# One batch's MLP split between two product forms, two exchange targets, and dense work laid out by units

## The chip, the cores and the metric

The kernel runs on one core of a Trainium2 chip, in one launch. The metric is the time of that launch in microseconds on the device; the table below has the median of three runs and one execution that was taken with the profiler. The five engines have their own instruction streams: PE (TensorE, with its weight loads as PEld), DVE (VectorE), ACT (ScalarE), POOL (GpSimd) and SP (SyncE), whose queue issues nearly all transfers.

## What is computed

A cross-attention block with its MLP, in float32: four batches of 512 tokens, 512 channels, 16 heads of 32, an MLP of 2048.

```python
residual = hidden_states
x = layer_norm(hidden_states, ln1_w, ln1_b)
q = (x @ q_w + q_b).reshape(B, LQ, H, HD).transpose(0, 2, 1, 3)
k = (encoder_hidden_states @ k_w + k_b).reshape(B, LK, H, HD).transpose(0, 2, 1, 3)
v = (encoder_hidden_states @ v_w + v_b).reshape(B, LK, H, HD).transpose(0, 2, 1, 3)
scores = jnp.einsum('bhqd,bhkd->bhqk', q, k) * scale
scores = jnp.where(mask, scores, mask_value)
attn = jax.nn.softmax(scores, axis=-1)
out = jnp.einsum('bhqk,bhkd->bhqd', attn, v)
out = out.transpose(0, 2, 1, 3).reshape(B, LQ, D)
out = out @ cproj_w + cproj_b
hidden = out + residual
residual = hidden
y = layer_norm(hidden, ln2_w, ln2_b)
y = jax.nn.gelu(y @ fc_w + fc_b, approximate=True)
y = y @ proj_w + proj_b
return residual + y
```

## The kernel before

**Units.** Attention runs over 16 groups `w` (four batches of four groups of four heads), and in each over four query tiles `qt` of 128 tokens. One (w, qt) is a unit, numbered u = 4w + qt from 0 to 63. `scores` has PE make four 128 x 512 score tiles in one four-bank PSUM tile, `sc`, of which there is one; DVE adds the mask and takes the row minimum (L244, scores are negated) into one of six `s` tiles; ACT takes the exponential with its sum (L248). `turn` has DVE transpose the four tiles in 32 x 32 blocks into `tb`. After the second unit of a pair (a half of a group's queries) DVE and ACT add the reciprocal sums, and `exchange` sends `tb` to a target tile, `pT`, by 16 transfers from SP's queue (`copies`), which move the blocks between partition quarters. `attend` then has PE multiply by the values (`av`) and DVE scale into `oT` (L327).

**Targets.** Pairs in `IN_G` go to `gt` and pairs in `IN_XE` to `xe`; all others go to the one `pT` tile, and then an exchange waits in a list until the pair before it has been attended (`held`). Pair p is attended before the scores of unit 2p + 4 (`LAG`), except for those in `AT`. `tb` has two buffers.

**Dense work.** Products of 128 x 512 x 512 are called chains: `prep_k`, `prep_q`, `prep_v` make a group's keys, queries and values, `cproj` is the attention's output projection of 128 tokens, `fc` and `proj` are the MLP's two halves in quarters of its 2048 channels. Each is four matmuls of 512 columns (sixteen of 128 in `prep_v`), a PSUM tile from a ring of four (`acc`) and an evacuation: by ACT for keys, queries, values and gelu, by DVE for cproj and proj. Lists `first[w]` and `later[w]` name the work of a group in order, with a cost (3.4 for a chain, 0.5 for a transpose step, 0 for vector work), and the loop spreads a group's list over its four units by an even share of that cost. `some(n)` takes the next n chains of the MLP. PE, DVE, ACT and SP run everything in the order in which it is written (a manual schedule).

**The MLP.** `NORMAL = 2`: batches 0 and 1 have all their MLP as chains, in the groups from 5 on and behind the loop, eight weight tiles in a ring (`load_mlp`). Batches 2 and 3 are done after attention in `last_mlps` with seven products of quarter blocks in place of eight (`fc_pair`, `project`): sums of weight blocks (`sum_wa`, `p_sums`), of activation blocks (`y_sums`, `g_sums`) and of results are made by DVE, ACT and POOL. A product there is two or sixteen matmuls of 256 columns.

**Layer norms.** `ln_stat` and `ln_norm` run on DVE, `ln_rs` on POOL; `ln_turn` transposes on PE and applies weight and bias on ACT (d = 0, 3) and DVE (d = 1, 2). `load_h` brings a batch's x again for the residual; batches that do not stay in SBUF go through DRAM (`xa`, `load_hid`).

The parts that order the work around the change are these:

```python
first[0] = [(CHAIN, lambda: prep_v(1))] + x2[:1] + [(CHAIN, lambda: prep_q(1))] + x2[1:2] + [k2] + x2[2:] + [k3, v2]
...
later[4] = c[:1] + x2[:1] + c[1:2] + x2[1:2] + c[2:3] + x2[2:] + c[3:] + stat(0, 0, 1, 2, 3) + rs(0)
first[5] = x3[:2] + [k] + x3[2:] + norm(0, 0, 1, 2, 3) + [v] + t2[:2] + [q] + t2[2:] + pb_(0) + some(5)
```

Of the kernel before, what the change touches and what calls it, by code (L numbers as in the profile page):

```python
# [43 lines left out]
P = 128  # L45
# [13 lines left out]
NORMAL = 2  # L59
LAG = 4  # L60
IN_G = (1, 3, 5, 7)
IN_XE = (29, 31)
AT = {5: 0, 7: 1, 9: 2, 11: 3, 13: 4, 15: 5, 17: 6}
# [10 lines left out]
def xattn_block(ctx: ExitStack, tc: tile.TileContext, x, encT, mask, q_w, k_w, v_w, c_w, fc_w, p_w, vecs, rows, out):  # L74
# [11 lines left out]
    one, two, kqp, five, six, fws = pools(att, one=1, two=2, kqp=4, five=5, six=6, fws=MW)  # L86
# [16 lines left out]

    S = {}
    Q = [nc.sync]
# [12 lines left out]
    def ln_rs(key):  # L118

        ve = small.tile([P, NT], F32, tag="ve", name=f"ve{key[0]}_{key[1]}")  # L120
        nc.gpsimd.tensor_scalar(ve, S["mv", key][:, :, 1], EPS, 1.0, ALU.add, ALU.mult)
        rs = small.tile([P, NT], F32, tag="rs", name=f"rs{key[0]}_{key[1]}")
        nc.gpsimd.tensor_tensor(rs, ve, nhalf, ALU.pow)
        S["rs", key] = rs

    def ln_norm(key, t, dst, src):
        nc.vector.tensor_scalar(
            dst, src, S["mv", key][:, t, 0:1], S["rs", key][:, t : t + 1], ALU.subtract, ALU.mult
        )

    def ln_turn(key, d, xn, dst):

        w, bi = (LN1W, LN1B) if key[0] == 1 else (LN2W, LN2B)
        tp = acc_tile(f"tp{key[0]}_{key[1]}_{d}")
        for t in range(NT):
            nc.tensor.transpose(tp[:, ts(t, P)], xn[t][:, ts(d, P)], ident)
        wd, bd = vec[:, w + d : w + d + 1], vec[:, bi + d : bi + d + 1]
        if d in (1, 2):
            nc.vector.tensor_scalar(dst[:, d, :], tp, wd, bd, ALU.mult, ALU.add)
        else:  # L140
            nc.scalar.activation(dst[:, d, :], tp, AF.Identity, bias=bd, scale=wd)  # L141
# [38 lines left out]
    def load_w(w, queue=None, names=("wk", "wq", "wv")):  # L180

        if w >= NW:
            return
        g = w % NG
        for n, src in (("wk", k_w), ("wq", q_w), ("wv", v_w)):
            if n in names:
                S[n, w] = two.tile([P, ND, P], F32, tag=n, name=f"{n}_{w}")
                (queue or Q[0]).dma_start(out=S[n, w], in_=src[:, g, :, :])

    def prep_k(w):  # L190
        b, g = divmod(w, NG)
        kT = kqp.tile([P, L], F32, tag="kT", name=f"kT_{w}")
# [7 lines left out]
    def prep_q(w):  # L200
        b, g = divmod(w, NG)
        qT = kqp.tile([P, L], F32, tag="qT", name=f"qT_{w}")
# [29 lines left out]
    def scores(w, qt):  # L232
# [8 lines left out]
        for h in range(HG):  # L241
            s = six.tile([P, L], F32, tag="s", name=f"s_{w}_{qt}_{h}")
# [93 lines left out]
    def stays(b, t):  # L336

        return b == 0 or b < B - 1 and t < 2

    def load_h(b, *ts_):  # L340
# [3 lines left out]
        for t in ts_:  # L344
            pool, tag = (hids, "hid") if stays(b, t) else (tiles, "xn")
            S["h", b, t] = pool.tile([P, D], F32, tag=tag, name=f"h_{b}_{t}")
# [8 lines left out]
    def cproj(b, t):  # L355
# [5 lines left out]
        if not stays(b, t):  # L361
            (nc.sync if b == B - 1 else nc.gpsimd).dma_start(out=S["xa", b][ts(t, P), :], in_=h)

# [30 lines left out]
    for b in range(NORMAL):  # L394
        for name, q in (("fc", 0), ("fc", 1), ("p", 0), ("fc", 2), ("p", 1), ("fc", 3), ("p", 2), ("p", 3)):
# [4 lines left out]
    count = [0, 0]  # L400

    def load_mlp():

        while count[0] < len(weights) and (count[0] < MW or weights[count[0] - MW][3] < count[1]):
            name, b, f, _ = weights[count[0]]
            w = fws.tile([P, D], F32, tag="mw", name=f"{name}w_{b}_{f}")
# [67 lines left out]

    def last_mlps():
# [5 lines left out]
        pb = last.tile([P, NP, 2, D], F32, tag="pb", name="pb")  # L481
        pt = last.tile([P, 3, NP, HL], F32, tag="pt", name="pt")
        hl = last.tile([P, NT, D], F32, tag="hl", name="hl")
        p1p, u2p, u3p = (last.tile([P, 2, HL], F32, tag=n, name=n) for n in ("p1p", "u2p", "u3p"))
# [13 lines left out]
        def p_sums(c):  # L498

            c = slice(c, c + 2)  # L500
            b11, b12, b21, b22 = (pb[:, c, k, j * HL : (j + 1) * HL] for k in range(2) for j in range(2))
            b_sums(b11, b12, b21, b22, pt[:, 0, c], pt[:, 1, c], b12, pt[:, 2, c])

# [5 lines left out]
        def fc_pair(b, c, sums):  # L509
# [25 lines left out]
            if c == 0:  # L535
# [9 lines left out]
            if c:  # L545
# [6 lines left out]
        def project(b, sums, turns, middle):  # L552
# [5 lines left out]
            def product(o, a, w, ts_=range(2)):  # L558
                for t in ts_:
                    for c in range(NP):  # L560
                        nc.tensor.matmul(o[:, t], a[:, c, ts(t, P)], w[:, c], start=(c == 0), stop=(c == NP - 1))  # L561
# [47 lines left out]

        y_sums(NORMAL)  # L610
        for t in range(NT):
            S["hid", B - 1, t] = hl[:, t]
        for b in range(NORMAL, B):
            for c in range(NP):
                if b == NORMAL:
                    for i in range(2):
                        nc.sync.dma_start(out=pb[:, c, i, :], in_=p_w[ts(2 * c + i, P), :])
                fc_pair(b, c, lambda: sum_wa(c + 1) if c + 1 < NP else None)
# [4 lines left out]
                if c % 2 == 0 and c:  # L623
                    g_sums(c - 2)

                if b + 1 < B:
# [8 lines left out]
            def sums(b=b):  # L635
                if b == NORMAL:
                    for c in range(0, NP, 2):
                        p_sums(c)
# [3 lines left out]
            def turns(b=b):  # L642
                if b + 1 < B:
                    run(turns2(b + 1))

# [5 lines left out]
            project(b, sums, turns, middle)  # L651
# [64 lines left out]
    load_h(0, *range(NT))  # L716
    nc.sync.dma_start(out=wc, in_=c_w)
# [8 lines left out]
    run(x1)  # L726
    make_mb(0)
# [10 lines left out]
    first[0] = [(CHAIN, lambda: prep_v(1))] + x2[:1] + [(CHAIN, lambda: prep_q(1))] + x2[1:2] + [k2] + x2[2:] + [k3, v2]  # L738
    first[1] = [(CHAIN, lambda: (prep_v(3), load_enc(1)))] + [q2, q3] + x3[:2]
    first[2] = [k4] + x3[2:] + [v4, q4] + A(5)[:1]  # L740
    first[3] = A(5)[1:] + A(6)
    mlp = []
    for p in range(NORMAL):
        mlp += FC(p, 0) + FC(p, 1) + PJ(p, 0) + FC(p, 2) + PJ(p, 1) + FC(p, 3) + PJ(p, 2) + PJ(p, 3)

# [27 lines left out]
    first[3] += cb(0)  # L773
# [3 lines left out]
    later[4] = c[:1] + x2[:1] + c[1:2] + x2[1:2] + c[2:3] + x2[2:] + c[3:] + stat(0, 0, 1, 2, 3) + rs(0)  # L777
    k, q, v = A(8)
    first[5] = x3[:2] + [k] + x3[2:] + norm(0, 0, 1, 2, 3) + [v] + t2[:2] + [q] + t2[2:] + pb_(0) + some(5)
    k, q, v = A(9)  # L780
    x1, x2, x3, x4 = inputs(3)
    first[6] = [k, q] + some(5) + [v] + x1
    k, q, v = A(10)
    first[7] = [k, q] + x2[:1] + some(3) + x2[1:2] + some(3) + [v]
# [5 lines left out]
    first[9] = [q] + some(2) + [k] + some(3) + [v]  # L790
    k, q, v = A(13)
    first[10] = [k, q] + some(5) + [v]
    k, q, v = A(14)
    t2 = turns2(1)
    first[11] = stat(1, 0, 1) + [k, q] + stat(1, 2, 3) + rs(1) + some(2) + norm(1, 0, 1) + some(1)
    first[11] += norm(1, 2, 3) + some(2) + t2 + pb_(1) + [v]

    k, q, v = A(15)
    first[12] = h_(2, 2, 3, 0, 1) + [k] + some(3)
    later[12] = cb(2) + C(2)  # L800
    first[13] = hid_(1, 2, 3) + [q] + some(3) + [v] + some(3)
    first[14] = some(5) + stat(2, 0, 1) + some(2) + stat(2, 2, 3) + rs(2) + some(1)
    first[15] = norm(2, 0, 1) + some(4) + norm(2, 2, 3) + some(4) + turns2(2) + pb_(2)

    for w in range(NW):
        if w and w % NG == 0:
            make_mb(w // NG)
        work, rest = first[w], later[w]
        share = sum(c for c, _ in work + rest) / NT
        due = 0.0  # L810
        for qt in range(NT):
# [7 lines left out]
            turn(w, qt)  # L819

# [6 lines left out]
        run(work + rest)  # L827
    exchange()

    load_h(B - 1, *range(NT))  # L830
# [3 lines left out]
    load_wa(0)  # L834
    run(some(2))
    attend(NW - 1, 1)
    run(some(2))
    load_wa(1)
    sum_wa(0)
    c_bias(B - 1)  # L840
    run(C(B - 1))
    load_hid(NORMAL, (2, 3))
# [46 lines left out]
```

## Time and profile before

| | us |
|---|---|
| median of three runs (820.71 to 821.26) | 820.94 |
| the profiled execution | 818.4 |
| its span, first to last instruction | 816.6 |
| PE busy | 798.2 |
| DVE busy | 546.8 |
| ACT busy | 354.6 |
| POOL busy | 90.5 |

Busy time is not a sum along a path: the engines run side by side, and a group's list decides what stands behind what. A line of the profile gives engine and source line (L244), what is written and read (`s<-sc,mb`), how often and how long, and what ended the idle time before it. `SPq` is SP's issuing queue, `PEld` a weight load. A matmul in float32 leaves two records. The clock that the throttle granted to TensorE is a column of the windows view, 1.00 being full speed.

### The profile page before, as it was taken

Reading aid. Unit: us, or ns where it says so; the run is one execution under the profiler, and the core shown is the slowest. Engines: PE = TensorE matmul, PEld = TensorE weight load, DVE = VectorE, ACT = ScalarE, POOL = GpSimd, SP = SyncE. Lnnn points to the kernel's source line nnn. Section 1 sums busy time; section 2 is a strip of 40 time slices with the busy share of each in tenths; the row PEclk is TensorE's granted clock in tenths of the full one; section 3 lists DMA queues with packets and bytes.
Section 4 is the critical chain, followed back from the end, with each engine's and each line's share of the span. In section 5 each row is a group of like instructions: output and inputs, shape, how many; then the busy total and the mean of one; then the engine's idle time right before and its main releaser. Section 6 shows DMA issues by size and latency. Waiting matters only on the chain.

```text
span 816.6 us, 11880 instructions
## 1 busy us (share of the span) xinstructions
PE 798.2 (98%) x3986; PEld 462.9 (57%) x3986; DVE 546.8 (67%) x1237; ACT 354.6 (43%) x766; POOL 90.5 (11%) x98
## 2 busy tenths in 40 slices
PE   9988999989999999999999999999999999999998
PEld 6453555444454554454454454344447888888887
DVE  3798977984675766667795766787327986368511
ACT  2465655256664743475336377557202330023200
POOL 1110003030000111000120210010201012200011
PEclk9999999999999999999999999999999999999999
DMA  9799898666777768686677576877635550023001
GB/s 328 247 222 241 220 245 251 186 155 168 179 200 199 186 164 237 160 222 159 175 214 196 148 199 157 201 176 197 176 116 181 180 168 13 26 78 91 0 14 40
DMA packets 60510, 137.15 MB, mean 168 GB/s; under 512 B 12401, under 2 KB 14577, under 8 KB 60321
## 3 DMA queue, kind: packets, MB, share of 16 engines
q1 hardware_dynamic: 59184, 132.95, 60.2%
q0 software_dynamic: 736, 2.29, 0.9%
q10 hardware_dynamic: 528, 1.14, 0.6%
q8 instruction: 32, 0.52, 0.3%
q14 instruction: 30, 0.24, 0.1%
HBM read 58.74 MB, written 6.29 MB: 80 GB/s over the span
## 4 chain that ended last, share of the span: by engine, by line
PE 84%; DVE 7%; DMA 5%; SPq 2%; ACT 1%; issue 1%; DVEq 0%; ACTq 0%
PE accf L417 14%; PE accp L427 13%; PE q L521 12%; PE sc L239 7%; PE av L322 7%; PE accv L217 5%; PE accc L359 5%; PE accq L205 4%; PE acck L195 4%; DVE s L244 3%; DVE tb L262 2%; SPq L305 2%; DMA xn<-x_dram 2%; PE q4p L561 2%; PE q3p L561 2%; PE q7p L561 2%
## 5 line engine op out<-in xcount | busy, mean ns | idle before, releaser
L248 ACT ACTIVATE s<-s,mn 128x512 f32<-128x512 f32 x256 | 181.6, 710 | 129.8 <-DVE mn L244 129.5
L244 DVE CUSTOM_DVE_ANT_0 s<-sc,mb 128x512 f32<-128x512 f32 x256 | 161.3, 686 | 60.2 <-PE sc L239 59.9
L262 DVE STREAM_TRANSPOSE tb<-s 128x512 f32<-128x512 f32 x224 | 146.3, 691 | 12.3 <-ACT s L248 9.5
L417 PE MATMUL accf<-yT,fcw 128*128 128x512 f32 x256 | 115.0, 598 | 0.0
L427 PE MATMUL accp<-pw,gt 128*128 128x512 f32 x256 | 115.0, 598 | 0.0
L417 PEld LDWEIGHTS accf<-yT,fcw 128*128 128x128 f32 x256 | 47.3, 190 | 65.0 <-issue 56.4
L427 PEld LDWEIGHTS accp<-pw,gt 128*128 128x128 f32 x256 | 47.2, 190 | 63.8 <-issue 61.3
L239 PE MATMUL sc<-kT,qT 32*128 32x512 f32 x512 | 73.9, 647 | 3.8 <-DVE mn L244 3.0
L217 PEld LDWEIGHTS accv<-wv,xe 128*128 128x128 f32 x512 | 58.7, 192 | 9.0 <-issue 5.7
L217 PE MATMUL accv<-wv,xe 128*128 128x128 f32 x512 | 60.7, 277 | 0.9 <-ACT xe L141 0.9
L521 PE MATMUL q<-ys,gt 128*128 128x256 f32 x256 | 60.1, 379 | 0.0
L195 PE MATMUL acck<-xe,wk 128*128 128x512 f32 x128 | 59.0, 603 | 0.0
L205 PE MATMUL accq<-xe,wq 128*128 128x512 f32 x128 | 58.4, 599 | 0.0
L359 PE MATMUL accc<-wc,oT 128*128 128x512 f32 x128 | 56.7, 597 | 0.0
L521 PEld LDWEIGHTS q<-ys,gt 128*128 128x128 f32 x256 | 48.6, 190 | 6.6
L322 PE MATMUL av<-pT,v 128*32 128x256 f32 x832 | 50.3, 382 | 2.1 <-DMA pT<-tb 1.6
L229 POOL TENSOR_TENSOR v<-v,row 128x512 f32<-128x512 f32 x16 | 20.4, 1275 | 270.4 <-ACT v L222 270.4
L248 ACT ACTIVATION_READ_ACCUMULATOR s<-s,mn 128x1 f32 x256 | 47.7, 186 | 0.0
L248 ACT ACT_TABLE_LOAD x21 | 26.9, 1283 | 46.3 <-DVE mn L244 46.3
L327 DVE TENSOR_TENSOR oT<-av,pT 128x256 f32<-128x256 f32 x26 | 11.0, 421 | 53.4 <-PE av L322 51.3
L521 PE MATMUL q<-yT,gt 128*128 128x256 f32 x192 | 46.3, 379 | 0.0
L525 ACT ACTIVATE ga<-uc,vec 128x256 f32<-128x256 f32 x32 | 16.3, 508 | 60.1 <-DVE uc L493 60.1
(108 smaller groups left out, 870.5 us busy)
## 6 DMA issues: line engine op xcount, KB each, us to landing
pT<-tb SPq DMA_DIRECT2D x416, 136.0 KB, 2.4
gt<-tb SPq DMA_DIRECT2D x64, 136.0 KB, 2.4
fcw<-fc_w_dram SPq DMA_DIRECT2D x32, 256.0 KB, 3.4
pw<-p_w_dram SPq DMA_DIRECT2D x32, 256.0 KB, 3.4
gt<-fc_w_dram SPq DMA_DIRECT2D x32, 256.0 KB, 2.9
wk<-k_w_dram SPq DMA_DIRECT2D x16, 256.0 KB, 3.7
xe<-encT_dram SPq DMA_DIRECT2D x16, 256.0 KB, 4.4
wv<-v_w_dram SPq DMA_DIRECT2D x16, 256.0 KB, 3.5
```

The lines of the kernel that those rows point to most:

```text
L195: nc.tensor.matmul(acc, S["wk", w][:, d, :], eT[:, d, :], start=(d == 0), stop=(d == ND - 1))
L205: nc.tensor.matmul(acc, S["wq", w][:, d, :], xT[:, d, :], start=(d == 0), stop=(d == ND - 1))
L217: nc.tensor.matmul(acc[:, ts(t, P)], eT[:, d, ts(t, P)], S["wv", w][:, d, :], start=(d == 0), stop=(d == ND - 1),)
L239: nc.tensor.matmul(sc[:, h, :], qT[r, ts(qt, P)], kT[r, :], start=True, stop=True)
L244: nc.vector.tensor_tensor_reduce(out=s, in0=sc[:, h, :], in1=S["mb", w // NG], scale=1.0, scalar=FMAX, op0=ALU.add, op1=ALU.min, accum_out=mn,
L248: nc.scalar.activation(s, s, AF.Exp, bias=mn, scale=-1.0, accum_out=sums[:, qt, h : h + 1])
L262: nc.vector.transpose(tv[:, q, h], S["ps", w, qt][h])
L322: nc.tensor.matmul(av[ts(h, HD), : 2 * P].rearrange(shape, **kw), v[:, t, ts(h, HD)], p[t][h], start=(t == 0), stop=(t == NT - 1),)
L359: nc.tensor.matmul(acc, S["oT", b][:, g, ts(t, P)], wc[:, g, :], start=(g == 0), stop=(g == NG - 1))
L417: nc.tensor.matmul(acc, S["fcw", b, f][:, d, :], S["yT", b][:, d, :], start=(d == 0), stop=(d == ND - 1))
L427: nc.tensor.matmul(acc, gT[q % 2][:, k, ts(t, P)], S["pw", b, q * FQ + k], start=(k == 0), stop=(k == FQ - 1))
L521: nc.tensor.matmul(o, a[:, k], y[:, k], start=(k == 0), stop=(k == 1))
```

## The change

It does these things together:

- Batch 1's MLP is split. Its first half (`FIRST = 2` quarters of the channels, fc and proj) stays as chains; the second half is done after attention by seven products, as four fc pairs and a `project` over four pairs, before batches 2 and 3. `project` and `fc_pair` take the range of pairs.
- The lists of groups 0 to 3, 5 and 11 to 15 become tuples with one list for each unit, which run just as they stand, and the other groups from 5 on have fewer MLP chains. Batch 2's attention projection and its second normalization's statistics stand elsewhere in that layout.
- From pair 24 on the exchanges go to `pT` and `xe` by turns, and these pairs are attended one unit later, before unit 2p + 5.
- Batch 1's first layer norm is applied on ACT, with a bias that POOL makes; its four evacuations of transposes are all on ACT.
- Batch 1's x is loaded ahead of batch 0's residual and of `wc`.
- One tile, `pbt`, holds keys, queries and the MLP's weight ring, and another, `ptt`, the score tiles and the q, k, v weights, with as many buffers as before; the seven-product weights of proj take the same places after attention. Batch 3's residual is loaded during unit 58, into places of dead keys and queries, and goes through DRAM for its second normalization.

```diff
-NORMAL = 2
+SPLIT = 1
+FIRST = 2
-IN_XE = (29, 31)
-AT = {5: 0, 7: 1, 9: 2, 11: 3, 13: 4, 15: 5, 17: 6}
+IN_XE = (25, 27, 29, 31)
+AT = {u: (u - 5) // 2 for u in (5, 7, 9, 11, 13, 15, 17, 53, 55, 57, 59, 61, 63)}
+BY_ACT = ((1, 1),)
...
     def ln_norm(key, t, dst, src):
+        if key in BY_ACT:
+            nc.scalar.activation(
+                dst, src, AF.Identity, bias=S["nm", key][:, t : t + 1], scale=S["rs", key][:, t : t + 1]
+            )
+            return
...
-        if d in (1, 2):
+        if d in (1, 2) and key not in BY_ACT:
...
+    def load_xn(b):
+
+        for t in range(NT):
+            S["h", b, t] = tiles.tile([P, D], F32, tag="xn", name=f"hn_{b}_{t}")
+            Q[0].dma_start(out=S["h", b, t], in_=S["xa", b][ts(t, P), :])
...
+    weights += [("p", SPLIT, FIRST * FQ + k, None) for k in range(MW)]
...
+        half = FIRST * FQ // 2
+        for b, pairs, new in (
+            (SPLIT, range(half, NP), ()), (SPLIT + 1, range(NP), range(half)), (SPLIT + 2, range(NP), ())
+        ):
...
     load_mlp()
-    load_h(0, *range(NT))
-    nc.sync.dma_start(out=wc, in_=c_w)
...
     run(x1)
+    load_h(0, *range(NT))
+    nc.sync.dma_start(out=wc, in_=c_w)
...
-    first[0] = [(CHAIN, lambda: prep_v(1))] + x2[:1] + [(CHAIN, lambda: prep_q(1))] + x2[1:2] + [k2] + x2[2:] + [k3, v2]
-    first[1] = [(CHAIN, lambda: (prep_v(3), load_enc(1)))] + [q2, q3] + x3[:2]
+    first[0] = [(CHAIN, lambda: prep_v(1))], [(CHAIN, lambda: prep_q(1)), k2] + x2[:1], [k3] + x2[1:2], [v2]
+    first[1] = [(CHAIN, lambda: (prep_v(3), load_enc(1)))] + x2[2:], [q2], [q3], x3[:2]
...
+    mlp += FC(SPLIT, 0) + FC(SPLIT, 1) + PJ(SPLIT, 0) + PJ(SPLIT, 1)
...
-    later[4] = c[:1] + x2[:1] + c[1:2] + x2[1:2] + c[2:3] + x2[2:] + c[3:] + stat(0, 0, 1, 2, 3) + rs(0)
+    later[4] = c[:1] + x2[:1] + c[1:2] + x2[1:2] + c[2:3] + x2[2:] + c[3:]
...
+    first[5] = (
+        [k, v] + stat(0, 0, 1, 2, 3) + rs(0) + x3 + norm(0, 0, 1, 2, 3), [q] + t2 + pb_(0), some(2), some(2)
+    )
...
-    first[12] = h_(2, 2, 3, 0, 1) + [k] + some(3)
-    later[12] = cb(2) + C(2)
-    first[13] = hid_(1, 2, 3) + [q] + some(3) + [v] + some(3)
-    first[14] = some(5) + stat(2, 0, 1) + some(2) + stat(2, 2, 3) + rs(2) + some(1)
-    first[15] = norm(2, 0, 1) + some(4) + norm(2, 2, 3) + some(4) + turns2(2) + pb_(2)
+    c = C(2)
+    first[12] = [k, q], cb(2) + [v], c[:2], c[2:]
+    first[13] = some(1), some(1) + stat(2, 0, 1), some(1) + stat(2, 2, 3) + rs(2), some(2)
+    first[14] = some(1) + norm(2, 0, 1), some(1) + norm(2, 2, 3), some(2) + h_(B - 1, *range(NT)), some(1)
+    first[15] = hid_(1, 2, 3) + some(1), some(1), some(1) + cb(B - 1), some(2)
...
+            if by_unit:
+                run(work[qt])
+                continue
...
-    load_wa(0)
+    load_wa(first_c)
     run(some(2))
+    p_sums(first_c)
     attend(NW - 1, 1)
-    run(some(2))
-    load_wa(1)
-    sum_wa(0)
-    c_bias(B - 1)
-    run(C(B - 1))
-    load_hid(NORMAL, (2, 3))
+    run(mlp)
+    load_wa(first_c + 1)
+    sum_wa(first_c)
+    c = C(B - 1)
+    run(c[:2])
+    p_sums(first_c + 2)
+    run(c[2:])
```

## The prediction

> **What bounds the kernel now.** I read the busy lines of the page first, then the chain that ended last, then a table of windows, and only then the timelines of the stretches in which the TensorE (PE) is not full.
>
> ```profile
> span 816.6 us, 11880 instructions
> PE 798.2 (98%) x3986; PEld 462.9 (57%) x3986; DVE 546.8 (67%) x1237; ACT 354.6 (43%) x766; POOL 90.5 (11%) x98
> ...
> 584.78 13.93 PE accp L427 x32
> ...
> 617.94 48.35 PE q L521 x224
> 666.28 6.91 PE q1p L561 x32
> ```
>
> PE is busy for 98% of the span, so PE work is the first currency. Four dense products in a row (accp, 32 records, two per matmul) take 13.93 us: 3.43 for each one that follows another, 3.63 for the first after scores. The seven-product form takes 48.35 for a batch's first half (fc) and 7 x 6.91 = 48.37 for its second: 96.7 where 32 dense products would be 110.
>
> ```profile
> 60.00:64.00 4.00, 1.56 (x28) 0.82 (x24) 4.00 (x13) 3.08 (x8) 0.00 (x0) 1.00 0.93 245
> 64.00:68.00 4.00, 4.00 (x28) 1.29 (x18) 2.76 (x6) 0.85 (x4) 0.00 (x0) 0.57 0.90 281
> ...
> 80.00:160.00 80.00, 79.49 (x525) 40.83 (x518) 68.80 (x172) 41.53 (x106) 11.85 (x11) 1.00 0.88 235
> 160.00:182.00 22.00, 18.38 (x128) 11.50 (x128) 18.29 (x44) 10.90 (x24) 7.39 (x7) 1.00 0.57 138
> 182.00:420.00 238.00, 237.00 (x1146) 109.38 (x1139) 161.83 (x385) 126.51 (x268) 17.32 (x19) 1.00 0.73 186
> 420.00:585.00 165.00, 164.28 (x784) 74.18 (x783) 115.04 (x262) 98.80 (x192) 18.20 (x18) 1.00 0.74 188
> ```
>
> Columns: window, length, busy time of PE, weight loads, DVE, ACT, POOL, granted clock, DMA share, GB/s. PE is full from 80 us on, but for 3.6 us in 160 to 182. Before 80 it has holes, and after one of them the clock falls to 0.57 for four microseconds. The timelines of SP's queue and of PE say what bounds it there:
>
> ```profile
> 50.67 10.33 SPq L305 DMA_DIRECT2D gt<-tb  x16
> ...
> 62.17 1.85 SPq L149 DMA_DIRECT2D xe<-encT_dram  x4
> 64.12 12.80 SPq L305 DMA_DIRECT2D pT<-tb  x16
> ...
> 62.97 2.55 PE L322 MATMUL av<-gt,v 128*32 128x256 f32 x32 [2.44 <-DMA gt<-tb]
> 65.45 2.09 PE L239 MATMUL sc<-kT,qT 32*128 32x512 f32 x8
> ```
>
> One exchange holds SP's queue for about 10.1 us (16 issues of 0.63), more when 256 KB loads stand just ahead, and lands some 2 us later. From 50.67 the queue never rests until 140.
>
> Last, the vector work of a unit (one query tile of one head group), from its own timeline:
>
> ```profile
> 38.69 0.66 DVE L244 CUSTOM_DVE_ANT_0 s<-sc,mb 128x512 f32<-128x512 f32 x1
> ...
> 41.11 2.49 DVE L262 STREAM_TRANSPOSE tb<-s 128x512 f32<-128x512 f32 x4
> 43.52 1.88 DVE L127 TENSOR_SCALAR xn<-xn,mv,rs 128x512 f32<-128x512 f32 x4
> 45.30 0.69 DVE L244 CUSTOM_DVE_ANT_0 s<-sc,mb 128x512 f32<-128x512 f32 x1
> ...
> 50.56 0.65 DVE L244 CUSTOM_DVE_ANT_0 s<-sc,mb 128x512 f32<-128x512 f32 x1
> ```
>
> Start to start, an even unit costs DVE 43.52 - 38.69 = 4.83 us and an odd one 50.56 - 45.30 = 5.26. That is below the sum of the mean durations, since instructions overlap. Other rows start to start: statistics 0.80 a tile, normalization 0.47, evacuation add 0.6, oT 0.4.
>
> **The change part by part.** I number units 4 x group + query tile, 0 to 63. Dense products per group are 5,3,4,5,7,8,8,9,8,8,8,8,8,8,8,8 before and 5,3,4,5,7,7,7,8,8,7,7,7,7,5,5,5 after: 16 fewer, with 7 left behind the loop in both.
>
> *Products.* Removed: 16 x 3.43 = 54.9. Added: four fc pairs, 48.35 / 2 = 24.2, and seven half-length products, 7 x 3.455 = 24.2. PE: **-6.5**. The 16 transposes of batch two's second normalization only move. Extra vector work of this half: y sums and half of the p sums lie under the last attention projection (13.9 us of PE). Where the half hands over to batch two, q4 now covers 3.45 instead of 6.91. In the trace DVE ends its joins, y_sums and sum_wa 5.6 us after q5; PE needs s4 3.45 + 1.73 = 5.2 after it. **+0.4** (0 to 1.5, if POOL's joins are late too).
>
> *The start.* Batch one's x is issued ahead of h and wc: about 19 instead of 22.76. Its statistics stand after unit 1 instead of unit 0, its normalization (1.8 on DVE) goes to ACT. The DVE wait for x at 28.4 to 30.3 goes. Then unit 2's scores are late next: PE reaches them at 35.27 either way, because unit 1 keeps its two products. From there I add: reduce of unit 2 at 36.5, statistics to 42.9, unit 3 from 42.9 to 48.2. The second exchange starts at 48.2 instead of 50.67, and the queue behind it shifts by 2.5: its enc loads, the third exchange, and av_1_0, which waits for it, at 76.3 instead of 78.83. q3 moves ahead of av_0_1 and fills the 2.44 us hole at 60.5. But the work ahead of av_1_0 is then done at 72.4: a hole of 3.9 us. ACT's four normalizations (4 x 0.6) end 0.8 after its next exp could start, which hides under the reduces.
>
> Here a rule is weighed. The row: after 2.44 us idle the clock was 0.57 for 4 us, and sc took 2.09 for 1.14, av 2.55 for 1.93, together 1.6. The Trainium skill (TensorE: Matmul & The Clock Gate, Part 1) says that only a whole idle window of about 3.4 us halves the clock. By the row the hole costs 1.6 more, by the rule, which needs the hole to span a free-running window, perhaps nothing. I take half to all of it: start **-1.5** (0 to -4).
>
> *Group 5.* Unit 20 waits 2.86 for ACT and unit 21 0.77, because four statistics (3.2) stand on DVE ahead of unit 20's reduces and ACT's exps follow them. They now stand behind. By the rows unit 20's reduces start at 160.05 instead of 163.3, and unit 22's scores at 179.4 instead of 181.34, with 1.6 of waits left on PSUM buffers that ACT frees. **-1.9** (0 to -3). The 0.72 wait among batch one's transposes at 424 should go as they are split: **-0.7** (0 to -0.7).
>
> *Seven-product groups.* An exchange of pair p with one target waits for oT of p-1, and av of p comes two units later. Needed: 0.55 + 10.1 + 2.0 = 12.65; 13.9 behind four loads. Two units with three products between them give PE 2 x 1.07 + 10.8 = 12.95. Such pairs are units 26-27, 38-39, 42-43 and 48-49, the last behind the four h loads: **+1.0** (0 to 3).
>
> *Groups 13 to 15.* A unit has one product (4.7 us, 6.5 with av) or two. Per group PE is 4 x 1.07 + 2 x 1.86 + 5 x 3.5 = 25.6. DVE: group 13 20.2 + two oT 0.8 + statistics 3.2 + five adds 3.0 = 27.2; groups 14 and 15 23.5 and 21.6. DVE may trail by about a unit, since scores wait only for the reduces before them; group 12 gives it 3 us of lead. Laid out unit by unit I find PE waiting under 1 us. SP per group: 20.2 + 2 to 6 of loads, 22 to 26. With two targets an exchange starts at once and has three units, about 18 us, for its 12.1; the shortest margin I find is av_14_1 with 0.7, av_14_0 with 2.7. Late: **+1.0** (0 to 6).
>
> Second rule, the one that speaks against the change. Units 57 to 62 each carry fc products, and each now has PE work of only 37.1 / 6 = 6.2.
>
> ```profile
> 523.60 1.28 ACT L248 ACT_TABLE_LOAD   x1 [3.06 <-DVE mn L244]
> 524.89 0.72 ACT L248 ACTIVATE s<-s,mn 128x512 f32<-128x512 f32 x1
> ...
> 527.84 1.28 ACT L418 ACT_TABLE_LOAD   x1
> 529.13 1.41 ACT L418 ACTIVATE gt<-accf,vec 128x512 f32<-128x512 f32 x2
> ```
>
> By these rows a unit with one gelu holds ACT 6.25 (even) or 6.9 (odd), reduce wait included: about PE's pace, trailing within the buffers. The Trainium skill (ScalarE: Activation LUTs, What ACT_TABLE_LOAD costs) puts a switch at some 2.66 us, a drain of 1.38 beside the load. Then ACT needs 9.3 a unit, 55 over these six, against 37 plus about 6 that it may trail: +12, and the sum below would be +4, slower. In the trace gelu starts 0.01 after the load's end and the load 0.02 after the accumulator read: no drain. I take the row.
>
> **Sum.** -6.5 - 1.5 - 1.9 - 0.7 + 0.4 + 1.0 + 1.0 = **-8.2**. The profiled execution was 818.4 (span 816.6 and 1.8 around it), 2.5 below the median 820.94; so span 808.4, profiled execution 810.2, median about **813**.
>
> **Rivals.**
> *The sum holds* (chance 0.64): 813. With the terms' bounds mostly independent its own range is 808 to 817.
> *SP's queue sets the pace of groups 13 to 15* (0.16). For: 22 to 26 us of issue in 25.6. Against: the third unit of lag. If each of six exchanges takes 11.3, as the one at 239.91 did behind four loads, 7.2 us come less the margins of 2: -3, about 818; with the start's gain lost as well, about 819.5.
> *The products alone count* (0.06): the reordering does not do what it says, at the start because the exchange of 64 to 77 keeps its place, in group 5 because ACT still frees the buffers late: -6.5 + 2.4 = -4.1, 817.
> *ACT becomes the bound in units 57 to 62* (0.14): the mechanism of the second rule, or any 0.5 us more per switch (6 us that it may trail over 11 switches), from which it decides; at the full 1.38 it is 825.
>
> **How the numbers follow.** About 0.2% (1.6 us) is what a measurement of this kernel can tell from no change. Faster: 0.64 + 0.06 + half of the queue's case = 0.78. Same: the rest of the queue's worse end, 0.06. Slower: ACT's case and a little of the queue's, 0.16. The range of 806.5 to 820 leaves out ACT's case and a gain beyond all bounds of the start.
>
> **What would show it.** The page: PE busy near 790 to 792 of a span near 808. The q products and q1p to q4p of batch one: 24.2 each. SP's second exchange issued near 48, av_1_0 near 76, with a granted clock under 1 just behind it. Unit 22's scores near 178. In the windows of groups 13 to 15, PE over 97% busy. Wrong would be: PE waiting there on DVE's reduces (ACT's case), or on a DMA of tb (the queue's), for more than 4 us; or statistics of batch one still waiting for x.

## The result, and the profile after

Median 819.37 us (20 runs, 815.00 to 823.10) against 821.25 for the kernel before in the same comparison (20 runs, 819.62 to 823.71): ratio 0.9973, 95% interval 0.9961 to 0.9985. So the change gains about 2 us, where 8 were forecast. The profiled execution of the changed kernel is the slowest of its 20 (823.1), and that of the kernel before lies below all of its 20 (818.4); the two traces therefore differ by +4.7 us in span, the medians by -1.9. Places are compared below by trace, sums by median.

The page, and then the windows view (columns as before: window, length, busy time of PE, weight loads, DVE, ACT, POOL, granted clock, DMA share, GB/s):

```profile
span 821.3 us, 11916 instructions
...
PE 796.2 (97%) x4082; PEld 483.6 (59%) x4082; DVE 557.9 (68%) x1279; ACT 355.5 (43%) x779; POOL 97.4 (12%) x110
```

```profile
64.00:68.00 4.00, 2.37 (x20) 1.21 (x20) 3.44 (x11) 2.33 (x7) 0.00 (x0) 1.00 1.07 308
...
76.00:80.00 4.00, 2.10 (x20) 1.14 (x24) 2.11 (x4) 0.00 (x0) 0.00 (x0) 0.50 0.94 269
...
184.00:188.00 4.00, 4.00 (x33) 1.40 (x26) 0.42 (x1) 0.00 (x0) 0.00 (x0) 0.59 0.00 0
...
420.00:585.00 165.00, 161.06 (x751) 75.31 (x750) 118.76 (x274) 75.17 (x164) 14.60 (x17) 0.99 0.74 198
516.00:520.00 4.00, 1.88 (x21) 1.20 (x25) 2.74 (x7) 3.97 (x9) 0.16 (x1) 0.80 0.99 252
```

The dip of the clock at 64 is gone; there are three new ones, near 76, 184 and 518, and they are the only places of the span with a clock under 0.995. PE is busy for 796.2, not the 790 to 792 forecast: with the same products, matmuls at a lower clock last longer; in u1 below, whose trace has one dip, PE is busy for 791.1. The view of PE's waits names what stands ahead of each dip:

```profile
PE av L362 <- DMA pT<-tb: 6.5, 3, 5.6
PE tp L176 <- ACT pbt L248: 4.2, 1, 4.2
...
PE av L362 <- DMA xe<-tb: 2.5, 1, 2.5
```

(total, times, longest.) The 5.6 is av_1_0 in unit 8, the 4.2 the last turn of batch zero's second norm in unit 21, the 2.5 av_14_1 behind unit 62. The chain that ended last shows that the seven-product half came as summed, one fc half and the first of seven products:

```profile
571.71 24.17 PE q L573 x112
595.88 3.45 PE q1p L613 x16
```

### The profile page after: what moved, and what is told of

It reads as the page before. It is cut to its first block, busy times and chain, and to the rows that moved or that the text cites. A ratio compares the mean times of both kernels' runs of the same rounds, so it can differ in the third digit from the quotient of the medians.

```text
span 821.3 us, 11916 instructions
## 1 busy us (share of the span) xinstructions
PE 796.2 (97%) x4082; PEld 483.6 (59%) x4082; DVE 557.9 (68%) x1279; ACT 355.5 (43%) x779; POOL 97.4 (12%) x110
## 4 chain that ended last, share of the span: by engine, by line
PE 81%; DVE 7%; SPq 6%; DMA 4%; issue 1%; ACT 0%; POOL 0%; DVEq 0%; POOLq 0%
PE q L573 15%; PE accp L479 8%; PE accf L469 7%; PE accc L403 7%; PE sc L279 6%; PE av L362 6%; SPq L345 6%; PE acck L235 6%; PE accq L245 5%; PE accv L257 5%; DVE ptt L284 3%; PE q5p L613 2%; PE q3p L613 2%; PE q7p L613 2%; PE q2p L613 2%; PE q1p L613 2%
## 5 line engine op out<-in xcount | busy, mean ns | idle before, releaser
L288 ACT ACTIVATE ptt<-ptt,mn 128x512 f32<-128x512 f32 x256 | 181.6, 711 | 145.0 <-DVE mn L284 144.9
L284 DVE CUSTOM_DVE_ANT_0 ptt<-sc,mb 128x512 f32<-128x512 f32 x256 | 161.0, 684 | 45.1 <-PE sc L279 44.9
L302 DVE STREAM_TRANSPOSE tb<-ptt 128x512 f32<-128x512 f32 x224 | 141.9, 683 | 9.6 <-DMA pT<-tb 5.2
L469 PE MATMUL accf<-yT,pbt 128*128 128x512 f32 x192 | 87.3, 601 | 0.0
L479 PE MATMUL accp<-pbt,gt 128*128 128x512 f32 x192 | 86.2, 599 | 0.0
L279 PE MATMUL sc<-pbt 32*128 32x512 f32 x512 | 73.5, 644 | 4.0 <-DVE mn L284 3.2
L257 PEld LDWEIGHTS accv<-ptt,xe 128*128 128x128 f32 x512 | 58.9, 192 | 9.7 <-issue 7.2
L257 PE MATMUL accv<-ptt,xe 128*128 128x128 f32 x512 | 60.6, 277 | 1.3 <-DVE xe L179 1.3
L235 PE MATMUL acck<-xe,ptt 128*128 128x512 f32 x128 | 59.4, 607 | 0.0
L245 PE MATMUL accq<-xe,ptt 128*128 128x512 f32 x128 | 58.3, 598 | 0.0
```

What stands on the lines that cost most here:

```text
L235: nc.tensor.matmul(acc, S["wk", w][:, d, :], eT[:, d, :], start=(d == 0), stop=(d == ND - 1))
L245: nc.tensor.matmul(acc, S["wq", w][:, d, :], xT[:, d, :], start=(d == 0), stop=(d == ND - 1))
L257: nc.tensor.matmul(acc[:, ts(t, P)], eT[:, d, ts(t, P)], S["wv", w][:, d, :], start=(d == 0), stop=(d == ND - 1),)
L279: nc.tensor.matmul(sc[:, h, :], qT[r, ts(qt, P)], kT[r, :], start=True, stop=True)
L284: nc.vector.tensor_tensor_reduce(out=s, in0=sc[:, h, :], in1=S["mb", w // NG], scale=1.0, scalar=FMAX, op0=ALU.add, op1=ALU.min, accum_out=mn,
L288: nc.scalar.activation(s, s, AF.Exp, bias=mn, scale=-1.0, accum_out=sums[:, qt, h : h + 1])
```

## The experiments

The theory after the two traces: the terms of products and of start are right, and three PE holes ate the gain, each with a dip behind it. The first rival: the two profiles differ by scatter between executions. The second: one resource sets the pace of all groups, so that removed holes only move. L numbers are the changed kernel's; "changed" is its median, 819.37. Ratios are to the kernel before on the same chip; two kernels a fifth of a per cent apart (1.7 us) are hardly told apart. The last column sets medians of different occasions beside each other; by the ratios the same differences are -3.2 for u1, -2.0 for e3, +2.0 for u2, -3.6 for f1 and -5.3 for b1 and b2, so read it to about 1 us.

| run | median us | ratio, 95% interval | minus changed |
|---|---|---|---|
| e1_q_early | 818.38 | 0.9962, 0.9947 to 0.9977 | -1.0 |
| e2_enc_other_queue | 819.00 | 0.9973, 0.9958 to 0.9987 | -0.4 |
| e3_h_behind_loop | 816.92 | 0.9949, 0.9932 to 0.9966 | -2.5 |
| e4_all_three | 817.03 | 0.9939, 0.9918 to 0.9960 | -2.3 |
| u1_group5_before | 815.11 | 0.9934, 0.9909 to 0.9959 | -4.3 |
| u2_start_before | 820.98 | 0.9997, 0.9980 to 1.0013 | +1.6 |
| u3_one_target | 830.31 | 1.0108, 1.0083 to 1.0134 | +10.9 |
| e5_norm_on_act | 816.94 | 0.9945, 0.9922 to 0.9968 | -2.4 |
| f1_fill | 815.03 | 0.9929, 0.9905 to 0.9952 | -4.3 |
| p1_products | 817.13 | 0.9950, 0.9933 to 0.9967 | -2.2 |
| b1_group5_and_h | 813.59 | 0.9909, 0.9877 to 0.9941 | -5.8 |
| b2_v4_before_av | 813.80 | 0.9909, 0.9885 to 0.9933 | -5.6 |
| f2_fill_all_three | 815.18 | 0.9919, 0.9899 to 0.9939 | -4.2 |
| b3_group5_h_fill | 812.35 | 0.9892, 0.9867 to 0.9917 | -7.0 |

**Group 5: put back (u1), and two repairs (e1, e5).**

```diff
# u1 (in place of e1's line that goes, below)
+    later[4] = ... + c[3:] + stat(0, 0, 1, 2, 3) + rs(0)
+    first[5] = x3[:2] + [k] + x3[2:] + norm(0, 0, 1, 2, 3) + [v] + t2[:2] + [q] + t2[2:] + pb_(0) + some(4)
# e1
-        [k, v] + stat(0, 0, 1, 2, 3) + rs(0) + x3 + norm(0, 0, 1, 2, 3), [q] + t2 + pb_(0), some(2), some(2)
+        [k, v] + stat(0, 0, 1, 2, 3) + rs(0) + x3 + [q] + norm(0, 0, 1, 2, 3), t2 + pb_(0), some(2), some(2)
# e5
+BY_ACT = ((1, 1), (2, 0))
+        [k, v] + stat(...) + rs(0) + x3 + [q] + norm(...) + t2, pb_(0) + some(1), some(2), some(1)
```

> The changed kernel with group 5 put back to the order of the kernel before: batch zero's statistics at the end of group 4, group 8's products and the transposes between them. The prediction's own working made this move worth 1.9 us, so by it this kernel is slower by 1.9 than the changed kernel's 819.4 (821.3, ratio 0.9996). Theory now: the new order let one late evacuation of ACT empty PE for 4.15 us, with a clock dip behind it; the old one had 2.86 + 0.77 in two short waits. From unit 20 to unit 22 the old order took 21.3 us in its trace, the new 25.7, so this kernel is faster by about 4 (2 to 5): 815.5, ratio 0.993.

> The changed kernel, with group 8's query product moved from unit 21 to the end of unit 20, ahead of the normalization of batch zero: its evacuation then stands on ACT ahead of the exps of unit 21. Theory (three PE holes ate the gain, each with a clock dip behind it): in the trace of the changed kernel the last of the four transposes of unit 21 waited 4.15 us for that evacuation and 0.57 for the norm, and the av after it took 3.64 for 1.93. Unit 22's scores should start near 181 instead of 186.4, the granted clock in 180 to 188 be 1.00, and the median fall by about 4 us (2.5 to 6) against the changed kernel's 819.4, to about 815.5 (0.9975 - 0.005 = 0.9925 of the kernel before). Rival (the differences between the two profiles are scatter between executions, and the groups are paced by VectorE anyway): under 1 us, ratio 0.996 to 0.998.

> The changed kernel with batch zero's second normalization and the evacuation of its transposes on ACT (as the change does it for batch one's first), group 8's query product and the transposes ahead of unit 21's scores, and one of unit 22's products in unit 21. Theory (VectorE, full from 144 to 182 us in the trace of the changed kernel, holds back unit 21's reduces, and through ACT's order the PSUM buffers): unit 22's scores after one product more at 183 to 184 us, that is 180 without it, instead of 186.4; no wait over 2 us and no dip in 170 to 190; median faster by 5 us (3 to 7) than the changed kernel, 814.5 (ratio 0.992). The kernel with the query product alone moved only exchanged the wait for another of 3.8 us, on a buffer that ACT empties behind the exps of unit 21. Rival (the waits there just move again): under 1.5 us, ratio 0.995 to 0.997.

u1 measured 815.11, the theory's 815.5 and not the prediction's 821.3. PE's timeline in the changed kernel, in unit 21, and ACT's beside it:

```profile
176.42 1.20 PE L176 MATMUL tp<-ident,xn 128*128 128x128 f32 x9 [0.57 <-DVE xn L167]
181.78 1.12 PE L176 MATMUL tp<-ident,xn 128*128 128x128 f32 x4 [4.15 <-ACT pbt L248]
182.82 3.64 PE L362 MATMUL av<-pT,v 128*32 128x256 f32 x32
186.39 1.57 PE L279 MATMUL sc<-pbt 32*128 32x512 f32 x8
```

```profile
177.01 0.72 ACT L288 ACTIVATE ptt<-ptt,mn 128x512 f32<-128x512 f32 x1 [5.37 <-DVE mn L284]
...
181.04 0.68 ACT L248 ACTIVATE pbt<-accq,qb 128x512 f32<-128x512 f32 x1
```

The query product and the four turns of batch zero need five PSUM tiles, and the ring has four; so the last turn waits until ACT has emptied accq. That stands behind the exps of unit 21, these behind DVE's reduces, and these behind four statistics (166.8 to 170.0), the wait for rs and four normalizations (172.55 to 176.3). These took twice the time that they take in u1 and in the kernel before (1.91):

```profile
172.55 3.82 DVE L167 TENSOR_SCALAR xn<-h,mv,rs 128x512 f32<-128x512 f32 x4 [1.03 <-POOL rs L153]
173.17 5.55 POOL L374 TENSOR_TENSOR h<-h,row 128x512 f32<-128x512 f32 x4 [0.66 <-DVE xn L167]
```

The first two take 0.55 each; the last two, which run beside POOL's bias adds, 1.5 each. This is so in all nine traces with the statistics in this place and the normalization on DVE. In u1, in the kernel before and in the four others with the old order no add of POOL runs beside it, and all four take 0.54. By these rows about 1.9 of the 4.15 us comes from there (an estimate, 3.82 - 1.91, since DVE goes on to the reduces without a pause); no run separates it from the order of the statistics. The av behind the hole takes 3.64 instead of 1.93. In u1 PE waits 2.80 for ACT in unit 20 and 1.28 in unit 22, without a dip, and unit 20 to unit 22 takes 178.19 - 157.32 = 20.9 us instead of 186.39 - 160.73 = 25.7, of which 0.5 is one more turn that stands there in the new order.

e1 missed: the wait was the same length almost, one instruction later.

```profile
180.97 3.40 PE L362 MATMUL av<-pT,v 128*32 128x256 f32 x32 [3.81 <-ACT yT L181]
```

With accq emptied early, the four turns fill the ring instead, and av waits for the first of them, which ACT empties behind the same exps. e5 takes the normalization off DVE and gained 2.4, less than u1 and than its theory's 3 to 7: four waits of 0.38 to 1.48 for ACT's normalized tiles took the place, with a dip behind them (clock 0.50 from 173.0 to 176.4) that the theory excluded. So it is not a buffer alone: what stands ahead on DVE, POOL and ACT in this unit decides.

**The last groups: h behind the loop (e3), one target (u3).**

```diff
# e3
-    first[14] = ..., some(2) + h_(B - 1, *range(NT)), some(1)
-    first[15] = hid_(1, 2, 3) + some(1), some(1), some(1) + cb(B - 1), some(2)
+    first[14] = ..., some(2), some(1)
+    first[15] = hid_(1, 2, 3) + some(1), some(1), some(1), some(2)
     exchange()
+    load_h(B - 1, *range(NT))
...
+    c_bias(B - 1)
     c = C(B - 1)
# u3
+IN_XE = (29, 31)
+AT = {u: (u - 5) // 2 for u in (5, 7, 9, 11, 13, 15, 17)}
```

> The changed kernel, with the four loads of batch three's x (h) and their bias add moved from units 58 and 62 to where the kernel before has them, behind the loop. Theory: exchange 29 starts at 501.5 instead of 503.0 and takes 10.1 to 11 us instead of 13.1, av_14_1 no longer waits 2.49 us, and the av behind it takes 1.93 instead of 3.43; the median falls by about 4 us against the changed kernel (2 to 4.5), to 815.5 (ratio 0.9925). Rival (SP's queue is at its limit from group 13 on whatever is loaded there): the wait moves to the next exchange, av_15_0 or av_15_1 waits instead, gain under 1 us.

> The changed kernel with one exchange target in groups 12 to 15, as before: only pairs 29 and 31 keep the second target, and the attention products of pairs 24 to 29 follow one unit sooner. An exchange then starts only after the oT of the pair before, needs 0.55 + 10.1 + 2.0 = 12.65 us, up to 15.5 behind loads, and PE has 12.8 us of work in two units. Theory (the second target is needed once the groups are this short): six to seven exchanges, each with 0 to 3 us of waiting and some with a clock dip: slower by 6 us (3 to 12) than the changed kernel, 825 (ratio 1.005). Rival (SP's queue, not the target, is what limits): the same within 1.5 us.

SP's queue in the changed kernel, then in e3:

```profile
499.54 1.49 SPq L461 DMA_DIRECT2D pbt<-p_w_dram  x3
501.12 1.80 SPq L391 DMA_DIRECT2D pbt<-x_dram  x4
503.03 13.08 SPq L345 DMA_DIRECT2D xe<-tb  x16
```

```profile
494.41 1.50 SPq L461 DMA_DIRECT2D pbt<-p_w_dram  x3
496.75 10.47 SPq L345 DMA_DIRECT2D xe<-tb  x16
```

Without the four loads the exchange starts at the end of its turn and takes 2.6 us less, av_14_1 waits for nothing and takes 1.93, and no later av waits: -2.5, at the low end of the theory's 2 to 4.5, and the wait did not move on. The theory's 4 took the hole of one trace for the usual one; in five others with the h loads in place av_14_1 waits 0.88 to 2.77. u3 cost 10.9, nearly twice the forecast: its av wait 13.1 us in sum for transfers to `pT`, of which 4.15 in unit 8; a wait of 4.25 ahead of unit 58 has a dip behind it. u3 attends these pairs one unit earlier too, so it prices target and lag together: without them the lighter groups lose more than the whole change gains.

**The start: undone (u2), and the encoder loads on another queue (e2); the three repairs together (e4).**

```diff
# u2
+BY_ACT = ()
     load_mlp()
+    load_h(0, *range(NT))
+    nc.sync.dma_start(out=wc, in_=c_w)
...
# e2
-            queue(b).dma_start(out=eT[:, d, :], in_=encT[b, ts(d, P), :])
+            (nc.gpsimd if b == 1 else queue(b)).dma_start(out=eT[:, d, :], in_=encT[b, ts(d, P), :])
# e4: e1, e2 and e3 together
```

> The changed kernel with the start (groups 0 to 3, order of the first loads, batch one's normalization on VectorE) as in the kernel before. The prediction made the new start worth 1.5 us (0 to 4): by it this kernel is slower by 1.5, 820.9 (ratio 0.9991). Theory now: the new start gains about 4.5 us up to unit 8 and loses 5.3 there, since the exchange it waits for ends no earlier and the idle time drops the clock; this kernel is within 1 us of the changed one, 818.5 to 820.5 (ratio 0.996 to 0.999), with a hole of about 2.4 us at unit 7 instead of 5.6 at unit 8.

> The changed kernel, with the four loads of batch one's encoder rows issued from GpSimd's queue instead of SP's, so that they no longer stand between the second and the third exchange. Theory: the third exchange starts near 60.3 instead of 62.2 and takes 10.1 to 10.5 us instead of 13.8, because the loads run earlier, beside the second exchange (from 45 us on); av_1_0 starts near 72 to 73 instead of 77.9, with no clock dip behind it; the median falls by 4 to 7 us against the changed kernel, to 813 to 815 (ratio 0.990 to 0.993). Rival (the bandwidth of the 1 MB, not its place in the queue, is what costs): the second exchange takes 3 us longer instead, the third starts 3 us later, and the gain is under 1.5 us.

> The three edits together (query product of group 8 early, batch one's encoder loads on GpSimd's queue, batch three's h behind the loop). Theory: the three add up, as each takes away a hole at another place: -10 to -15 us against the changed kernel, 805 to 809 (ratio 0.980 to 0.985), with the granted clock at 0.998 or more over the whole span, and the scatter between executions smaller than the changed kernel's 815.0 to 823.1. Rival (one resource is the bound of all groups, so removing holes only moves the waits): less than half of the sum of the three single gains.

u2, which has `first[0]` to `first[3]` of the kernel before too: +1.6, the prediction's 1.5 and not the theory's "within 1" (though 818.5 to 820.5 is not far, and the interval reaches into both). In its trace av_0_1 waits 2.49 and av_1_0 3.03 where the changed kernel has 5.6 in one. e2 missed:

```profile
65.94 3.64 PE L362 MATMUL av<-gt,v 128*32 128x256 f32 x32 [3.85 <-DMA ptt<-v_w_dram]
```

GpSimd issued the loads at 53.9, behind its bias adds, beside the second exchange. That exchange's last issue ended at 59.40 (59.10 in the changed kernel), but its last transfer landed at 65.74 instead of 60.92. (The row names a weight load; that landed at 66.81, after av had begun.) The third exchange did become shorter (11.3), and the hole came one pair earlier, dip included. So here the 1 MB cost about the same beside the second exchange, from another queue, as ahead of the third on SP's. e4 then gained only e3's part: the other two had only moved their holes.

**Useless work in the holes (f1, f2).**

```diff
# f1
+    def fill(n):
+        dummy = acc_tile(f"fill_{count[1]}")
+        for i in range(n):
+            nc.tensor.matmul(dummy, ident, wc[:, i % ND, :], start=(i == 0), stop=(i == n - 1))
-    first[2] = [k4], x3[2:] + [v4], [q4], [k5]
+    first[2] = [k4] + do(lambda: fill(3)), x3[2:] + [v4], [q4], [k5]
-    first[15] = ..., some(1) + cb(B - 1), some(2)
+    first[15] = ..., some(1) + cb(B - 1) + do(lambda: fill(2)), some(2)
# f2: f1, and in ln_turn
+        for t in range(7 * NT if key == (2, 0) and d == 2 else 0):
+            nc.tensor.transpose(tp[:, ts(t % NT, P)], xn[t % NT][:, ts(d, P)], ident)
```

> The changed kernel with PE kept busy in two of its three holes by products whose sum nobody reads: three of 512 columns (2.6 us) ahead of av_1_0 in unit 8, two (1.7 us) ahead of av_14_1 in unit 62; the hole of unit 21 is left. Nothing waits less for a transfer. Theory (a hole costs its length and then a clock dip of about 1.6 us, because the clock falls after idle time): the av behind both places takes 1.93 us instead of 3.64 and 3.43, the clock in 72 to 84 and in 516 to 524 is 1.00, and the median falls by 3 us (1.5 to 3.3) to about 816.5 (ratio 0.994). Rival (the dip comes with the pressure of the transfers or at times of its own, not from idle time): the dips stay, and the median stays within 1 us.

> The changed kernel with PE kept busy in all three holes by work that nobody needs: the two fills of the run with two holes filled, and in unit 21 the transposes of the third turn repeated seven times into their own tile (3.4 us of the 4.15 that the fourth turn waits). No wait gets shorter. Theory (the clock behind a hole is a cost of its own, beside the hole): against the run with two holes filled (815.0) the av of unit 22 takes 1.93 instead of 2.84, the clock in 176 to 184 is 1.00, and the median falls by 1.0 to 1.7 us, to 813.5 to 814 (ratio 0.991 to 0.9915); so of the 4.3 us that group 5's order cost, 1 to 1.7 are the clock and the rest the wait. Rival (group 5 costs its wait alone, the clock there is made good by later waits): 815 (ratio 0.993).

f1's PE in unit 8:

```profile
72.28 2.74 PE L793 MATMUL fill<-wc,ident 128*128 128x512 f32 x6
77.02 1.93 PE L362 MATMUL av<-pT,v 128*32 128x256 f32 x32 [2.00 <-DMA pT<-tb]
```

The transfer still lands near 77, PE does 4.6 us more work, and the kernel is 4.3 us faster: av takes 1.93 instead of 3.64, and behind unit 62 1.93 instead of 3.43. This is the clearest run of the study: it speaks against dips that come with the transfers, and shows the clock behind a hole as a cost of its own. f2 took the third dip away in its trace (against f1's, av 1.93 instead of 2.84, and unit 20 to 22 in 23.6 us instead of 24.9), and its granted clock is 0.998 to 1.000 in all six runs, where the changed kernel's twenty have 0.990 to 0.998. But its median is no lower than f1's (815.18 against 815.03; by ratios 0.9919 against 0.9929): what the third dip is worth stays undecided. The scatter became smaller with the fills: 2.1 us from the fastest to the slowest of f2's six runs and 1.6 of f1's, which keeps one dip, against 8.1 of the changed kernel's twenty.

**What is left, and the best version (p1, b1, b2, b3).**

```diff
# p1: u1, u2 and e3 together       # b1: u1 and e3 together
# b2: b1, and
+    first[2] = [k4] + x3[2:] + [v4], [q4], [k5], [q5]
+    first[3] = [v5], [k6], [q6], [v6] + do(lambda: c_bias(0))
# b3: b1, and f1's fill(3) in unit 8
```

> What is left of the change when its start and its group 5 are put back to the kernel before and batch three's h is loaded behind the loop again: the seven-product half, the second exchange target and the lighter groups. The prediction's sum for these is -6.5 + 0.4 - 0.7 + 1.0 = -5.8 (the +1.0 of the last groups is left out, since h is out of the way): 815.5 (ratio 0.993). By the single runs, if they add (819.4 + 1.6 - 4.3 - 2.5): 814.2 (ratio 0.9915). Rival (the products themselves are worth less than 6.5, and the rest of the change was needed to collect them): 817.5 or more, ratio above 0.9955.

> The changed kernel with group 5 as in the kernel before and batch three's h loaded behind the loop: the two edits that each gained alone (-4.3 and -2.5 against the changed kernel). If they add: 812.6 (ratio 0.9895); of the three holes only the one of unit 8 is left, so at most one clock dip, granted clock 0.997 or more, and a scatter between executions of at most 4 us, where the changed kernel has 8. Rival (with group 5 earlier, the transfers of the last groups come later against PE and a new wait takes the place): 814.5 or more (ratio above 0.992).

> The kernel of the run before it, and group 4's value product and two turns moved from unit 9 to unit 8, ahead of av_1_0, with the products behind them each one unit earlier. Theory: the hole of unit 8 (2.5 to 5.6 us, the landing of the third exchange) is filled with 4.7 us of work that is needed anyway, no dip follows, and the exchanges behind it allow 2 of the 5 us to be kept: 2 to 3 us faster than the kernel of the run before, 810 (ratio 0.9865). Rival (from 48 to 123 us SP's queue never rests and sets the pace, so that a filled hole opens again at the next exchange): within 1 us, with waits of av on transfers in units 10 to 16.

> The changed kernel with group 5 as before and batch three's h behind the loop (813.6 as it was run), and three products whose sum nobody reads ahead of av_1_0 in unit 8. Theory: the wait for the third exchange stays, the clock dip behind it goes: 1 to 1.6 us faster, 812 to 812.5 (ratio 0.9885 to 0.989), granted clock 0.998 or more in nearly every execution. Rival (the next exchanges from unit 10 to 17 set the pace there, so that the start gains nothing): 813.6 (ratio 0.991).

b1: 813.59, between the two limits named; its interval of 0.9877 to 0.9941 holds both (0.9895 and 0.992), so whether the two gains add fully stays open. Its scatter (6.7 us) missed the forecast of 4, and its trace has two dips instead of one: a 2.80 us wait for ACT in unit 20, which u1 has too, brought one here and not there. p1: 817.13, between the prediction's 815.5 and the rival's 817.5 but nearer to the rival's: its interval (0.9933 to 0.9967) leaves out 0.993 and the 0.9915 of adding single runs. The new start, worth 1.6 in u2, is worth 3.5 between p1 and b1: single gains do not add exactly. That dips come with some waits and not with others may be why; no run shows it. b2: no gain over b1. Its unit 8 has no wait, but the av ahead of unit 18 waits 2.58 for an exchange to `gt` and is followed by a dip: the rival's case, one unit behind the 10 to 16 that it named. b3 keeps the wait for the third exchange and only takes the dip: 812.35, 1.2 less than b1 and within its noise, the fastest of all. b1 is the version without useless work; it beats both kernels.

Of the two first rivals, scatter alone is out: the intervals of u1 and f1 lie wholly below the changed kernel's. That removed holes only move is true of e1, e2 and b2, and false of u1 and e3.

## Why the prediction was wrong, point by point

The direction was right and the size was not: -8.2 forecast, -1.9 measured.

*Products, -6.5 and +0.4: held as PE time.* 24.17 and 7 x 3.45 for the half, as summed, and 0.46 of waiting for DVE (L501) where the hand-over was put at 0.4.

*Start, -1.5: held in the median (u2: 1.6), and in its places.* The second exchange was issued at 48.45 (forecast 48.2). av_1_0 came at 77.90 (forecast 76.3) in this trace, where the third exchange took 13.8 us behind the 1 MB; the traces of seven programs that are the same up to there have it at 74.8 to 77.9, so this landing itself scatters by 3 us, with the forecast inside.

*Group 5, -1.9: the step that failed.* The text says "unit 22's scores at 179.4 instead of 181.34, with 1.6 of waits left on PSUM buffers that ACT frees". They came at 186.39. The sum followed DVE to unit 20's reduces, which did start earlier (1.2 us behind their scores instead of 4.5), and stopped there. The statistics were not gone: with the normalization they stood ahead of unit 21's reduces instead, ACT's exps followed these, and the buffer of the fourth turn followed the exps: 4.15 + 0.57 of waiting, and a dip. The normalization was also taken at 0.47 a tile, from a row without POOL beside it; beside POOL's adds it took 3.82 in all. u1 sizes the term: +4.3 (+3.2 by the ratios) instead of -1.9. That this 6.2 is as large as the whole shortfall of 6.3 is partly luck, since the term of groups 13 to 15 fell short too and single gains do not add exactly.

*Batch one's transposes, -0.7, and seven-product groups, +1.0: no contradiction.* No wait of PE stands at the split transposes, and of the four pairs of units two have a wait, 0.31 and 0.56.

*Groups 13 to 15, +1.0: too low.* The shortest margin was named rightly (av_14_1, 0.7; PE's sum of 25.6 a group comes to 25.5), but the exchange was costed at 12.1 from issue to landing; behind three weight loads and four h loads it started 1.6 late and took 13.1 to issue alone. The price in the median is e3's 2.5 (2.0 by the ratios).

Leaving out group 5's term and the h loads, the prediction's terms give -6.5 - 1.5 - 0.7 + 0.4 + 1.0 = -7.3, and b1, which leaves out just these two, measured -7.5 against the kernel before (821.12 to 813.59). The other terms hold as a sum, but not one by one: without the start they give -5.8, and p1 measured -4.0 (-2.7 to -5.5 by its interval), while the start gave -3.5 between p1 and b1 where -1.5 was forecast. The two misses cancel.

*The rivals.* "SP's queue sets the pace" gave 818 to 819.5, and the median is 819.4. The number fits for another reason: its mechanism was worth 2.5 at one exchange, not 7. "The products alone count" gave 817, which is p1's 817.13, but b1's start gains beyond it. "ACT becomes the bound" fell, by the ACT groups of table loads (count, busy, mean ns, idle before):

```profile
L470 ACT ACT_TABLE_LOAD x19 | 24.4, 1283 | 0.3
L288 ACT ACT_TABLE_LOAD x18 | 23.1, 1283 | 0.3
```

0.3 us of idle time before 19 loads is no drain of 1.38 each, which the Trainium skill (ScalarE: Activation LUTs, What ACT_TABLE_LOAD costs) puts beside the load; behind 28 of the 37 loads the next activation begins within 0.01 us, and behind the other nine ACT waits for DVE or PE. In units 57 to 62 PE waits 0.88 us for DVE's reduces and not for ACT.

*The clock.* The prediction priced one hole at 1.6 from its row of before, against the rule of the Trainium skill (TensorE: Matmul & The Clock Gate, Part 1) that a whole free-running idle window of about 3.4 us is needed. The price was right (an av of 3.64 for 1.93 is 1.7) but was booked for one place only, while it fell due at three. f1 puts two of them at 4.3 us in the median (3.6 by the ratios), where the two av rows give 3.2. Of the rule, the traces show the free-running window and not the need for a whole idle one (last section).

## What to carry to other kernels

When vector work is moved from ahead of one reduce to behind it, follow it to the next one: write down each engine's queue for at least two units on, with every PSUM tile and the instruction that frees it, since the wait comes back through the engine that is two steps away. An engine's price from a quiet row need not hold beside another engine: here two normalizations took 1.5 us beside POOL and 0.54 alone. Price each hole of PE at its length plus the dip behind it, and where a hole can't be closed, work that nobody needs in it was cheaper here than idling. A megabyte of loads beside a critical exchange cost about the same from another queue; whether another time helps was not run.

## What was not expected of the hardware

Over the sixteen traces, all of 14 PE holes from 3.8 us up were followed by a dip of the clock, and of 22 holes between 2.0 and 3.5 us 15 were: the same 2.80 us wait in unit 20 dipped in four kernels and not in u1, a hole of 2.11 dipped and one of 3.43 did not. The clock's own records in the traces say more. A dip lasts 3.41 or 6.83 us at a clock of 0.50, and within a trace all dips begin whole multiples of 3.41 us apart (74.67, 180.48 and 518.40 in the changed kernel: 31 and 99 of them). So time is cut into windows of 3.41 us that do not follow the program, and the clock of one goes by PE's work in the one before. Two such windows of the changed kernel, and two of e5 (columns as before):

```profile
71.25:74.67 3.42, 1.05 (x3) 0.19 (x1) 1.45 (x6) 3.29 (x9) 0.00 (x0) 1.00 0.90 210
74.67:78.08 3.41, 0.18 (x4) 0.21 (x8) 0.19 (x1) 0.00 (x0) 0.00 (x0) 0.50 0.94 228
...
70.61:74.02 3.41, 1.51 (x4) 0.38 (x2) 1.91 (x8) 3.41 (x10) 0.00 (x0) 1.00 0.98 223
74.02:77.43 3.41, 1.89 (x36) 1.15 (x36) 1.90 (x4) 0.34 (x1) 0.00 (x0) 1.00 0.90 271
```

In the changed kernel 1.05 us of work in a window halved the clock of the next, while PE was still idle; e5's hole of 3.43 falls into two windows with 1.51 and 1.89 us of work, and nothing follows. Over all sixteen traces, from 8 us to PE's end, each of the 29 windows at full clock with under 1.4 us of PE work was followed by one at 0.50, two of the six with 1.4 to 1.6 were, and none with more. So about 2 us of idle time in one window is enough here, in one hole or several: e5's four short waits dipped, and so did p1 at 49.0, behind a hole of 1.82. What looks like chance is where the windows lie against the program, which differs from trace to trace. The fills of f1 and b3 left 1.45 and 1.50 us of work in the poorest window of unit 8, just enough.

The time of one kernel scatters by 8 us with an unchanged program, and part of it lies in the granted clock of the execution: over a kernel's runs the two go together with a correlation of -0.92 in e1 and -1.0 in e4, but only -0.59 in the changed kernel, -0.41 in e2 and -0.31 in p1.
